# A four-layer megakernel: the last attention's projections copied out in pairs, two kinds of copy fixed to ACT, and roots of variances by bits in the last combine

## The chip, the cores and the metric

The kernel runs on one core of a Trainium2 chip. The metric is device time in microseconds (us) of one execution of the whole program. The time before is 2511.77 us, the median of three runs (2509.81 to 2514.41).

The engines are named as in the profile: PE (matrix products), DVE or VectorE, ACT (ScalarE), POOL (GpSimd) and SP (SyncE, which issues most transfers). PEld is PE's loading of weights, L12 is line 12 of the kernel before.

## What is computed

Four pairs of an attention and a feed-forward layer follow each other over x of 8 blocks x 256 tokens x 256 features, in fp32, each with a residual and a layer norm: `x = _layernorm(x + layer(x))`. The change touches the last pair. Its attention is a differential attention with 16 query heads and 4 key heads:

```
q = _rope((x @ Wq).reshape(b, s, H, 2 * D))
k = _rope((x @ Wk).reshape(b, s, KVH, 2 * D))
v = (x @ Wv).reshape(b, s, KVH, D)
scores = softmax(energy / np.sqrt(D))            # causal, two maps a head
diff = softmax(scores[:, 0] - lam * scores[:, 1])   # causal
att = einsum('bhqv,bvhd->bqhd', diff, v)
att = att * rsqrt(mean(att * att) + EPS) * rms_w * (1.0 - LAM_INIT)
return att.reshape(b, s, E) @ Wo
```

The last feed-forward layer routes each token to 4 of 32 experts (256 to 96 gated to 256), and sums the four results by their weights. Then come the last residual and norm:

```
m = jnp.mean(x); v = jnp.var(x)          # over the 256 features
return (x - m) / jnp.sqrt(v + 1e-5)
```

## The kernel before, in words

The eight blocks of 256 tokens stay in SBUF as `X[b]`, with a transposed copy `xT`. Layers run one after the other. For the last two (`attn3` and `ffn3`) the schedule is manual: each engine takes its instructions in the order in which the code emits them, so whatever stands in an engine's queue waits for all that is ahead of it there.

**Banks.** PSUM is divided by tags, two banks of 128 x 512 fp32 each: "a" and "s" (scores), "o" (attention's values) and "t" (everything else: projections, transposes, the output product). A product for a "t" bank waits until the bank's last content but one was copied out.

**The attention (`attn3`).** `project(b)` makes, for one block, the turned keys and queries and v. Each call of `turn` multiplies 128 columns of a weight with the block's 256 tokens into a "t" bank, and VectorE multiplies the result with a table of cosines or sines (L600). There are four for the keys (POOL adds the two parts of each half, L608), eight for the queries, and one product for v, which VectorE copies to `Vs` (L620). `project` is a generator: after each piece it yields. The first block's runs as a whole before the loop; that of block b + 1 is stepped inside the loop over block b's units.

A block has six units: two with the first 128 queries (qc = 0, two heads each in every group of four) and four with the other 128 (qc = 1, one head each, 256 keys). The loop over units is a software pipeline. In iteration n it emits, in this order:

- `factors` of unit n - 1: the reciprocal of its sums on DVE (L672), masking and the factor c on POOL (L677 to L683);
- `scores` of unit n: 32 or 16 products on PE (L642, two records each in the profile's count), mask products (L655), four maxima on DVE (L659), exponentials on ACT (L662);
- `values` of unit n - 3 on PE (L739); after the last unit of a query half the result is copied from "o" to `oS` by `self.copy`, which alternates between DVE (L118) and ACT (L120) over all its calls;
- one step of the projections;
- the first half of `differences` of unit n - 1: products and sums on DVE (L696), maxima (L700), then POOL (nmd L701, v L704);
- one more step of the projections, two if qc = 0;
- one step of `finish`, the end of an earlier block (transposes L756, att L761, the root mean square with POOL L778 to L788 and ACT L780 and L781, transposes L795, aT on ACT L799, output product L804, residual L164 and moments L183 and L184, norm L190, transposes L154);
- the second half of `differences`;
- one or two steps of the sorting of the last layer's first half, later three scatters on POOL (L954);
- `turned` of unit n - 2: transposes on PE (L721) into "t" and the second exponential on ACT (L723).

**The last layer (`ffn3`).** Tokens go to rows sorted by expert, in two halves of four blocks. The experts' loop runs over 63 tiles of 128 rows a half. `ffn3_combine(g, act, ahead)` then fetches, for each of the 8 tiles of 128 tokens of a half, four results by indirect DMA from POOL (L2048), and VectorE adds them by their weights to `X` (L2054). After each second tile it takes `moments`, and then the norm (L190) and the store of the block (L197). The combine of the first half runs inside the second half's experts; that of the second half runs alone at the end of the program, one tile of gathers ahead of the sums.

`moments` takes mean and variance on VectorE (L183, L184) and calls `rsqrt`, which is two instructions on POOL: multiply and add (L146), and a power of -0.5 (L147).

Of the kernel before, what the change touches and what calls it, by code (L numbers as in the profile page):

```python
# [10 lines left out]
F32 = mybir.dt.float32  # L11
BF16 = mybir.dt.bfloat16  # L12
I32 = mybir.dt.int32
U32 = mybir.dt.uint32
AF = mybir.ActivationFunctionType
ALU = mybir.AluOpType
AX = mybir.AxisListType

P = 128
NB = 8  # L20
T = 256
# [3 lines left out]
LN_EPS = 1e-5  # L25
# [14 lines left out]
class Model:  # L40
# [132 lines left out]
        self.normed(b, r, *self.moments(r))  # L173
        self.norm_done(b)

    def moments(self, r):

        nc = self.nc
        st = self.small.tile([P, 2, 6], F32, tag="bnst", name="bnst")
        mv = self.small.tile([P, 2, 2], F32, tag="bnmv", name="bnmv")  # L180
        rstd = self.small.tile([P, 2], F32, tag="rstd", name="rstd")
        for t in range(2):
            nc.vector.bn_stats(st[:, t, :], r[:, t, :])  # L183
            nc.vector.bn_aggr(mv[:, t, :], st[:, t, :])  # L184
        self.rsqrt(rstd, mv[:, :, 1], 1.0, LN_EPS)
        return mv, rstd

    def normed(self, b, r, mv, rstd):
# [364 lines left out]
    def attn3(self, w, act, keep, start=False, beside=None):  # L553
# [5 lines left out]
        nc = self.nc  # L559
# [4 lines left out]
        for i in range(2):  # L564
            pr = l[:, 2 * i, :]
            nc.vector.tensor_tensor(pr, pr, l[:, 2 * i + 1, :], ALU.mult)
            sm = act.tile([P, 16], F32, tag=f"lsm{i}", name="lsm", bufs=1)
# [17 lines left out]
        def project(b):  # L585

            if start:
                self.transpose_x(b)
            xT = self.xT[b // 2][:, :, (b % 2) * T : (b % 2 + 1) * T]
            qT = act.tile([P, 8, T], F32, tag="qT", name="qT")  # L590
            kT = act.tile([P, 2, T], F32, tag="kT", name="kT")

            def turn(out, wt, i, tab):
                ps = self.ps("t")[:, :T]
                for c in range(2):
                    nc.tensor.matmul(
                        ps, wt[:, c, i * P : (i + 1) * P], xT[:, c, :],
                        start=(c == 0), stop=(c == 1),
                    )
                nc.vector.tensor_tensor(out, ps, tab, ALU.mult)  # L600

            for a in range(2):
                k = kT[:, a, :]
                turn(k, w["wk"], 2 * a, w["ck"][:, a, :])
                yield
                x = act.tile([P, T], F32, tag="kh", name="kh", bufs=1)
                turn(x, w["wk"], 2 * a + 1, w["sk"][:, a, :])
                nc.gpsimd.tensor_tensor(k, k, x, ALU.add)  # L608
                yield
            for j in range(8):  # L610
                turn(qT[:, j, :], w["wq"], j, w["tq"][:, j % 2, :])
                yield
            ps = self.ps("t")[:, :128].rearrange("p (t n) -> p t n", t=2)
            for t in range(2):
                for c in range(2):
                    nc.tensor.matmul(
                        ps[:, t, :], xT[:, c, t * P : (t + 1) * P], w["wv"][:, c, :],
                        start=(c == 0), stop=(c == 1),
                    )
            nc.vector.tensor_copy(  # L620
                Vs[b % 2][:, :, :, 0:16], ps.rearrange("p t (s d) -> p t s d", s=4)
            )
            qTs[b], kTs[b] = qT, kT
            yield

        class Unit:
# [102 lines left out]
            def values(u):  # L729

                V = Vs[u.b % 2]
                if u.h0 == 0:
                    oT[u.b, u.qc] = self.ps("o").rearrange("p (h q) -> p h q", h=4)
                o = oT[u.b, u.qc]
                for c in range(1 + u.qc):
                    for s in range(4):
                        out = o[32 * s : 32 * s + 32, u.h0 : u.h0 + u.nh, :]
                        x = u.p[s] if u.qc == 0 else u.p[s][:, c : c + 1, :]
                        nc.tensor.matmul(  # L739
                            out, V[:, c, s, :], x, start=(c == 0), stop=(c == u.qc)  # L740
                        )
                if u.h0 + u.nh == 4:
                    oS = keep.tile([P, 4, P], F32, tag=f"oS{u.qc}", name="oS", bufs=1)
                    self.copy(oS, o)
                    oSs[u.b, u.qc] = oS
                    if u.qc == 1:
                        done.append(finish(u.b))
# [71 lines left out]
        projections, ends, done = [], [], []  # L819

        def step(queue, n=1):

            while n and queue:
                if next(queue[0], StopIteration) is StopIteration:
                    queue.pop(0)
                else:
                    n -= 1

        for _ in project(0):
            pass  # L830
# [3 lines left out]
        for n in range(len(units) + 3):  # L834

            def at(back):
                return units[n - back] if 0 <= n - back < len(units) else None

            u, last = at(0), at(1)
            if u and u.qc == 0 and u.h0 == 0:  # L840
                step(projections, 100)
                if u.b + 1 < NB:
                    projections.append(project(u.b + 1))
            if last:
                last.factors()
            step(others)
            if u:
                u.scores()
            if at(3):
                at(3).values()  # L850
            step(projections)
            halves = last.differences() if last else iter(())
            next(halves, None)
            step(projections, 2 if u and u.qc == 0 else 1)
            step(ends)
            next(halves, None)
            next(halves, None)
            if not self.scattering:
                step(others, 2)
            if at(2):  # L860
                at(2).turned()
            ends += done
            done.clear()
# [1168 lines left out]
    def ffn3_combine(self, g, act, ahead):  # L2032


        nc = self.nc
        first, n = GROUPS[g]
        wt, slots, _ = self.sorted[g]
        ys, rs = {}, {}
        for t in range(2 * n + ahead):
            i = t - ahead  # L2040
            b = first + i // 2
            if t < 2 * n:
                ys[t] = act.tile([P, 4, D], F32, tag="yk", name="yk", bufs=4)
            if i >= 0 and i % 2 == 0:
                rs[b] = act.tile([P, 2, D], F32, tag="rk", name="rk", bufs=3)
            for k in range(4):
                if t < 2 * n:
                    nc.gpsimd.indirect_dma_start(  # L2048
                        out=ys[t][:, k, :], out_offset=None, in_=self.outs[g],
                        in_offset=bass.IndirectOffsetOnAxis(ap=slots[:, t, k : k + 1], axis=0),  # L2050
                    )
                if i >= 0:
                    r = rs[b]
                    nc.vector.scalar_tensor_tensor(  # L2054
                        r[:, i % 2, :], ys[i][:, k, :], wt[:, i, k : k + 1],
                        self.X[b][:, i % 2, :] if k == 0 else r[:, i % 2, :], ALU.mult, ALU.add,
                    )
                yield
            if i >= 0 and i % 2 == 1:
                m = self.moments(rs[b])  # L2060
                yield
                self.normed(b, rs[b], *m)
                self.norm_done(b)
                yield
# [228 lines left out]
```

## Time and profile before

| what | us |
|---|---|
| median of the three runs | 2511.77 |
| the profiled execution | 2512.97 |
| its span, first to last instruction | 2511.2 |
| the last attention, about | 1745 to 2216 |
| the last layer's experts, about | 2216 to 2452 |
| the last combine and store | 2452 to 2511 |
| PE busy | 2192.5 (87%) |
| DVE busy | 1431.1 (57%) |
| ACT busy | 1047.5 (42%) |
| POOL busy | 916.9 (37%) |

The profile is of one execution. A row of the timeline gives start, duration, engine, line, operation and tiles; in brackets the time that the engine sat idle before it and what ended that. In the table of waits a row names who waited for whom, then the total, the number of times and the longest. The durations of two instructions that follow each other on VectorE overlap a little, so starts tell more than durations. The mean granted clock of PE was 0.949.

### The profile page before, as it was taken

The page shows a single profiled execution, that of the slowest core. Times are in us where ns is not written, and L with a number is a line of the kernel's source. Part 1 is how long each engine was busy: PE and PEld are TensorE (multiplying, and loading weights), DVE is VectorE, ACT ScalarE, POOL GpSimd, SP SyncE. Part 2 cuts the span into 40 slices and gives each one's busy share as a digit, 9 for nine tenths or more (in the row PEclk, how much of TensorE's full clock was granted, in tenths as well). Part 3 has the DMA queues.
Part 4 walks back from the last instruction along what each step waited for, and adds up shares of the span by engine and source line. Part 5 has one row for each costly group of instructions (what it writes and reads, how often), then busy time and mean ns, then how long its engine had stood idle before and what let it go on. Part 6 is the DMA issues. An engine that isn't in the chain of part 4 may idle for free. (4 is left out here: it accounts for less than half of the span.)

```text
span 2511.2 us, 36255 instructions
## 1 busy us (share of the span) xinstructions
PE 2192.5 (87%) x11960; PEld 1494.2 (60%) x12016; DVE 1431.1 (57%) x3593; ACT 1047.5 (42%) x3005; POOL 916.9 (37%) x1725
## 2 busy tenths in 40 slices
PE   7998899999999999999999999998877777678990
PEld 4554697756666666666664465555555554457780
DVE  4556486754544543544465454565888878645463
ACT  1334365453544544544432112221766755644450
POOL 1222443343433323333312321000566557833555
PEclk9999999999999999999999999999999978789995
DMA  5000411100000100000260011002000000145663
GB/s 160 1 1 1 165 44 40 59 5 4 3 3 8 47 1 1 1 1 1 74 206 1 1 51 52 1 0 103 1 2 1 1 1 26 41 125 172 213 212 96
DMA packets 92309, 120.76 MB, mean 48 GB/s; under 512 B 9757, under 2 KB 79582, under 8 KB 91102
## 3 DMA queue, kind: packets, MB, share of 16 engines
q1 hardware_dynamic: 82270, 95.75, 11.8%
q0 software_dynamic: 8192, 21.11, 2.8%
q8 instruction: 100, 1.64, 0.3%
q10 hardware_dynamic: 1664, 1.57, 0.2%
q14 instruction: 83, 0.68, 0.1%
HBM read 67.53 MB, written 50.88 MB: 47 GB/s over the span
## 5 line engine op out<-in xcount | busy, mean ns | idle before, releaser
L1391 POOL TENSOR_SCALAR p<-p,rs 128x128 f32<-128x128 f32 (+1 forms) x256 | 104.2, 425 | 294.7 <-DVE rs L1389 290.4
L1381 ACT ACTIVATE p<-ps_s,nm,rq 128x128 f32<-128x128 f32 (+1 forms) x256 | 128.0, 507 | 152.2 <-DVE nm L1379 152.2
L1309 ACT ACTIVATE sq<-ps_a 128x512 f32<-128x512 f32 x126 | 76.0, 603 | 227.2 <-PE ps_a L1301 226.9
L146 POOL TENSOR_SCALAR rsq<-bnmv 128x2 f32<-128x2 f32 x64 | 13.6, 212 | 377.5 <-DVE bnmv L184 369.9
L662 ACT ACTIVATE e<-ps_a,nm 128x128 f32<-128x128 f32 (+1 forms) x256 | 105.9, 435 | 107.7 <-DVE nm L659 98.4
L1310 DVE TENSOR_REDUCE ssk<-sq 128x4 f32<-128x512 f32 x64 | 43.8, 686 | 172.9 <-ACT sq L1309 172.9
L704 POOL TENSOR_SCALAR v<-e,r,nmd 128x128 f32<-128x128 f32 (+1 forms) x256 | 134.6, 537 | 10.0
L1301 PE MATMUL ps_a<-w_a_wq,xT 128*128 128x512 f32 x256 | 122.3, 600 | 12.4 <-DVE k L1323 9.4
L721 PE MATMUL ps_t<-ident,v 128*128 128x128 f32 x384 | 69.2, 317 | 61.7 <-DVE qT L600 29.4
L1301 PE MATMUL ps_a<-w_a_wv,xT 128*128 128x512 f32 x256 | 120.6, 593 | 1.0 <-ACT q L1334 1.0
L1981 PE MATMUL ps_a<-w_f_gup,xTg 128*128 x504 | 111.5, 345 | 11.4 <-DVE xTg L1975 6.9
L696 DVE SCALAR_TENSOR_TENSOR e<-e,c 128x128 f32<-128x128 f32 (+1 forms) x256 | 105.1, 460 | 25.5 <-POOL c L683 25.3
L1310 DVE TENSOR_REDUCE ssq<-sq 128x4 f32<-128x512 f32 x64 | 43.9, 686 | 129.8 <-ACT sq L1309 129.8
L1301 PE MATMUL ps_a<-w_a_wk,xT 128*128 128x512 f32 x248 | 116.5, 593 | 0.0
L1429 PE MATMUL ps_o<-w_a_wo,attT 128*128 128x256 f32 x512 | 111.8, 379 | 0.0
L662 ACT ACTIVATE e<-ps_s,nm 128x128 f32<-128x128 f32 (+1 forms) x256 | 106.8, 452 | 0.0
L1429 PEld LDWEIGHTS ps_o<-w_a_wo,attT 128*128 128x128 f32 x512 | 96.7, 190 | 12.8
L1163 DVE SCALAR_TENSOR_TENSOR yg<-ps_t,xg,yg 128x128 f32<-128x128 f32 x266 | 93.1, 350 | 12.7 <-PE ps_t L1152 3.9
L1368 PE MATMUL ps_s<-kT,qT 128*128 128x256 f32 (+1 forms) x512 | 100.3, 329 | 0.0
L721 PEld LDWEIGHTS ps_t<-ident,v 128*128 128x128 f32 x384 | 50.2, 163 | 81.4 <-issue 31.4
L1415 PE MATMUL ps_o<-pT,V 128*128 128x256 f32 x256 | 79.5, 392 | 19.2 <-ACT pT L120 19.2
L1981 PEld LDWEIGHTS ps_a<-w_f_gup,xTg 128*128 128x128 f32 x504 | 82.4, 197 | 22.2 <-ACT yg L2011 10.6
(410 smaller groups left out, 6041.7 us busy)
## 6 DMA issues: line engine op xcount, KB each, us to landing
rows<-zero SPq DMA_DIRECT2D x42, 384.0 KB, 4.5
xg<-rows SPq DMA_DIRECT2D x42, 384.0 KB, 5.1
outs<-yg SPq DMA_DIRECT2D x42, 384.0 KB, 3.7
w_f_gup<-in_f_gup SPq DMA_DIRECT2D x8, 768.0 KB, 8.6
w_f_w<-in_f_w SPq DMA_DIRECT2D x8, 512.0 KB, 6.3
w_f_down<-in_f_down SPq DMA_DIRECT2D x8, 384.0 KB, 8.3
w_f_up<-in_f_up SPq DMA_DIRECT2D x5, 512.0 KB, 7.3
lrows<-zero SPq DMA_DIRECT2D x12, 204.0 KB, 5.7
```

Of the source, the lines that this page charges most:

```text
L662: nc.scalar.activation(e[:, s, j * nk : (j + 1) * nk], sc[s][:, j, :], AF.Exp, bias=nm[:, s, j : j + 1], scale=1.0, accum_out=sums[:, s, j ...
L696: nc.vector.scalar_tensor_tensor(d[:, s, h, :], u.e[:, s, h, 1, :], u.c[:, s, h : h + 1], d[:, s, h, :], ALU.mult, ALU.add,)
L704: nc.gpsimd.tensor_scalar(u.v[:, s, h, :], d[:, s, h, :], u.r[:, s, h, 0:1], nm[:, s, h : h + 1], ALU.mult, ALU.add,)
L721: nc.tensor.transpose(ps[:, s, c, :], x, self.ident)
L1163: nc.vector.scalar_tensor_tensor(acc[j], y, c, acc[j], ALU.mult, ALU.add)
L1301: nc.tensor.matmul(ps, self.xt(u.b, t, c), w[which][:, c, u.cols], start=(c == 0), stop=(c == 1),)
L1310: nc.vector.tensor_reduce(out, sq, AX.X, ALU.add)
L1368: nc.tensor.matmul(sc[:, j, :], u.qT[:, h0 + j, qc * P : (qc + 1) * P], u.kT[:, h0 + j, 0:nk], start=(j == 0), stop=False,)
L1381: nc.scalar.activation(u.p[qc][:, h0 + j, :], sc[:, j, :], AF.Exp, bias=nm[:, j : j + 1], scale=r[:, j : j + 1], accum_out=u.sums[qc][:, h ...
L1391: nc.gpsimd.tensor_scalar(u.p[qc][:, j, :], u.p[qc][:, j, :], ri[:, j : j + 1], 1.0, ALU.mult, ALU.mult,)
L1429: nc.tensor.matmul(y[:, t, :], attTs[b][:, h, t * P : (t + 1) * P], w["wo"][:, h, :], start=(h == 0), stop=(h == 15),)
L1981: nc.tensor.matmul(ps, xT[j][:, c, :], w["gup"][:, bass.ds(er[j], 1), c, :].rearrange("p o f -> p (o f)"), start=(c == 0), stop=(c == 1),)
```

## The change

In `project`, `turn` takes several column blocks. It puts two of them side by side into one bank and VectorE multiplies all 512 columns with the two tables in one instruction. So the keys take two steps in place of four (one addition of 512 columns on POOL in place of two of 256), the queries four in place of eight. The loop takes the second step of projections only in units with qc = 0. The copy of v and every copy of `oS` are made by ACT; since `self.copy` alternates, its other calls may fall on the other engine than before. In the last combine the roots are computed by VectorE: a first guess by integer operations on the bits and three Newton rounds, 15 instructions with the addition of eps; only the last block's root stays on POOL.

```diff
+    def rsqrt_bits(self, out, v, eng):
+
+        n = v.shape[1]
+        half = self.small.tile([P, 4], F32, tag="nm", name="rsh")[:, :n].bitcast(I32)
+        self.nc.vector.tensor_scalar(half, v.bitcast(I32), 1, None, ALU.arith_shift_right)
+        self.nc.vector.tensor_scalar(
+            out.bitcast(I32), half, -1.0, float(0x5F3759DF), ALU.mult, ALU.add
+        )
+        t = self.small.tile([P, 4], F32, tag="sm", name="rst")[:, :n]
+        for _ in range(3):
+            eng.tensor_tensor(t, out, out, ALU.mult)
+            eng.tensor_tensor(t, t, v, ALU.mult)
+            eng.tensor_scalar(t, t, -0.5, 1.5, ALU.mult, ALU.add)
+            eng.tensor_tensor(out, out, t, ALU.mult)
+
-    def moments(self, r):
+    def moments(self, r, by_bits=False):
...
-        self.rsqrt(rstd, mv[:, :, 1], 1.0, LN_EPS)
+        if by_bits:
+            v = self.small.tile([P, 4], F32, tag="rs", name="rsv")[:, :2]
+            nc.vector.tensor_scalar(v, mv[:, :, 1], LN_EPS, None, ALU.add)
+            self.rsqrt_bits(rstd, v, nc.vector)
+        else:
+            self.rsqrt(rstd, mv[:, :, 1], 1.0, LN_EPS)
...
-            def turn(out, wt, i, tab):
-                ps = self.ps("t")[:, :T]
-                for c in range(2):
-                    nc.tensor.matmul(
-                        ps, wt[:, c, i * P : (i + 1) * P], xT[:, c, :],
-                        start=(c == 0), stop=(c == 1),
-                    )
+            def turn(out, wt, tab, *cols):
+                ps = self.ps("t").rearrange("p (a t) -> p a t", a=2)
+                for a, i in enumerate(cols):
+                    for c in range(2):
+                        nc.tensor.matmul(
+                            ps[:, a, :], wt[:, c, i * P : (i + 1) * P], xT[:, c, :],
+                            start=(c == 0), stop=(c == 1),
+                        )
                 nc.vector.tensor_tensor(out, ps, tab, ALU.mult)
-            for a in range(2):
-                k = kT[:, a, :]
-                turn(k, w["wk"], 2 * a, w["ck"][:, a, :])
-                yield
-                x = act.tile([P, T], F32, tag="kh", name="kh", bufs=1)
-                turn(x, w["wk"], 2 * a + 1, w["sk"][:, a, :])
-                nc.gpsimd.tensor_tensor(k, k, x, ALU.add)
-                yield
-            for j in range(8):
-                turn(qT[:, j, :], w["wq"], j, w["tq"][:, j % 2, :])
+            turn(kT, w["wk"], w["ck"], 0, 2)
+            yield
+            kh = act.tile([P, 2, T], F32, tag="kh", name="kh", bufs=1)
+            turn(kh, w["wk"], w["sk"], 1, 3)
+            nc.gpsimd.tensor_tensor(kT, kT, kh, ALU.add)
+            yield
+            for j in range(0, 8, 2):
+                turn(qT[:, j : j + 2, :], w["wq"], w["tq"], j, j + 1)
                 yield
...
-            nc.vector.tensor_copy(
+            nc.scalar.copy(
                 Vs[b % 2][:, :, :, 0:16], ps.rearrange("p t (s d) -> p t s d", s=4)
             )
...
-                    self.copy(oS, o)
+                    nc.scalar.copy(oS, o)
...
-            step(projections, 2 if u and u.qc == 0 else 1)
+            if u and u.qc == 0:
+                step(projections)
...
-                m = self.moments(rs[b])
+
+                m = self.moments(rs[b], g == 1 and i < 2 * n - 1)
```

## The prediction

> **What bounds the kernel now.** I read the chain that ended last first, in order of time. It reaches back over the last 300 us only; its end is a run of gathers on POOL, and with the stretch around one root it reads:
>
> ```profile
> 2467.90 0.94 POOL yk L2048
> 2468.84 0.30 issue
> 2469.14 0.94 POOL yk L2048
> 2470.09 0.07 issue
> 2470.16 0.20 POOL rsq L146
> 2470.36 0.07 issue
> 2470.43 0.72 POOL rstd L147
> 2471.15 0.19 issue
> 2471.34 1.17 POOL yk L2048
> 2472.52 0.30 issue
> 2472.82 0.96 POOL yk L2048
> 2473.78 0.31 issue
> 2474.08 0.95 POOL yk L2048
> ```
>
> From 2455 us on, the time is 32 gathers, one every 1.25 us, and three such breaks in between; the last gather starts at 2497.79, lands 2.8 us later, and the last block's norm and store follow. VectorE only has to keep up.
>
> For the other part of the change, the last attention (1745 to 2216 us), I cut the time into stretches: us, then PE, PEld, DVE, ACT, POOL busy, clock, DMA.
>
> ```profile
> 1860.00:1920.00 60.00, 46.31 (x429) 31.93 (x431) 51.63 (x116) 41.29 (x165) 37.77 (x92) 0.97 0.01 2
> 2100.00:2160.00 60.00, 43.08 (x357) 29.51 (x358) 45.91 (x101) 40.23 (x165) 50.89 (x102) 0.86 0.12 40
> ```
>
> To 2100 VectorE is the fullest (86%), PE close behind (77%); then POOL, which also issues scatters, is (85%). Nobody is full, so the waits matter. VectorE's own waits in the stage (total, times, longest) and PE's for a bank that VectorE empties (1800 to 2040 us):
>
> ```profile
> DVE e L696 <- POOL c L683: 25.3, 16, 6.1
> DVE nm L659 <- PE ps_a L655: 16.8, 17, 2.3
> DVE V L620 <- PE ps_t L616: 12.3, 7, 5.2
> DVE res L164 <- PE ps_t L804: 8.8, 5, 1.8
> ```
>
> ```profile
> PE ps_t L721 <- DVE qT L600: 20.9, 16, 2.4
> ```
>
> So PE's in-order queue stands behind the second projection of a unit, which VectorE copies out only after the first half of the differences, and the next scores stand behind that; then VectorE waits for those (16.8 us).
>
> **Tail (roots by bits).** Three of the four roots leave POOL. From the 12th gather's start (2469.14) to the 14th's (2472.82) are 3.68 us, where two periods are 2.50: 1.18 us a root. About 0.1 of that may stay, since the gather beside the norm's two L190 instructions took 1.17 us, and the very first one, with VectorE idle, 1.07. So 1.08 to 1.18, three times: 3.2 to 3.5; I take 3.3. VectorE gets 15 small instructions a block instead (one for eps, two for the first guess, three rounds of four). Small dependent ones start 0.21 us apart in the sorting code (L908 at 2072.87, L909 at 2073.08): 3.2 us a block. Cover: two tiles are gathered in 10.0 us and cost VectorE 8 x 0.51 (L2054) + 1.2 moments + 3.2 + 0.7 (L190) = 9.2. At the end: new last gather at 2456.64 + 30 x 1.25 = 2494.2, landing at 2497.0; the third block's sums end near 2487.5, moments 2488.6, bits 2491.8, norm 2492.5, four sums of tile 6 2494.6, three of tile 7 2496.3. 0.7 us of slack; an instruction of 0.26 us instead of 0.21 would use it up. The last root stays on POOL, where nothing queues behind it: no change.
>
> A rule speaks against this. The row: L2054 reads two SBUF tensors for 0.48 us beside gathers (2464.49, the gather at 2464.16), and the next gather still comes 1.25 us later. The Trainium skill, "SBUF — State Buffer", section "SBUF: two separate sides": VectorE instructions in a two-port mode, or with two SBUF inputs against a GpSimd one that reads SBUF, hold a port pair that GpSimd shares; the loser is blocked, descriptors of POOL's DMAs included, until about 115 ns after VectorE's end (the page's next section). Twelve of the 15 have two SBUF inputs. By the rule (an estimate from that page) 12 x (0.19 + 0.115) = 3.7 us a block would be added where 1.18 is removed: the tail 7.5 us longer. By the row nothing. I take the row, since it is the same engine pair and the same DMA; the other end stays in the range.
>
> **Attention: VectorE's queue.** 84 projections of 256 columns are copied out in the loop (12 for each of seven blocks; the first block's 12 come before it). L600 lasts 0.415 us, but two in a row start 0.33 apart; 512 columns of PSUM (L659) start 0.60 apart. So a pair saves 0.06, 42 pairs 2.5 us, not the 0.14 that durations suggest. V's copy: 7 x 0.25 = 1.8. Half of the 16 oS copies were on VectorE: 8 x 0.60 = 4.8. Sum 9.1 us off VectorE. ACT gets 8 x 0.62 (L120 oS) + 8 x 0.3 = 7.4 us; it waits 98 us for L659's maxima in this stage, and the copies stand behind the unit's 8 or 16 exponentials and ahead of the two of L723. They add a wait on ACT for PE's products, which are done while the exponentials run; behind it queue L723's results, and PE's values for those. Without that cover a copy costs its 0.3 or 0.62 us. A general rule says otherwise (the Trainium skill, "ScalarE: Activation LUTs", "Rules for kernel authors": simple elementwise work belongs on VectorE, up to about three times faster per element in bf16): 3 x 0.68 would be 2.0 us a copy, 16 us on ACT. The rows of oS itself (DVE 680 ns, ACT 586 to 622) decide: fp32 from PSUM is no slower on ACT. POOL's two adds of 0.74 us become one of 512, about 1.4 by the same rate, all of it in a block's first unit; the second half's nmd and v queue behind it, but POOL waits 93 us for L700 in the stage. Uncovered it would be 0.7 us a block.
>
> **Attention: the order.** A unit with one query half (qc = 1) now has one pair, in the first place; qc = 0 has two pairs instead of three turns. Two effects, opposite in sign.
> Later: PE works 1.0 us on a turn (two turns 1891.19 to 1893.18), 2.0 on a pair, and VectorE can't start on half of it. Where VectorE reaches the place, against the end of both turns: 1866.33 / 1866.6, 1874.72 / 1874.8, 1892.81 / 1893.18, and one more like it, 1909.13 / 1909.04. So 0 to 0.4 us, about 0.25 for each of four first places a block: +1.0.
> Earlier: in qc = 1 units nothing of a projection is left after the first half, so PE's turning (1895.21, after 1.21 us of wait) no longer waits for it. I replayed the block from 1863 to 1917 by these rows. The unit from 1872.4 gains 1.3, as its scores come before VectorE needs them (it waited 1.55 there); the next two lose 0.15 and 0.3 (VectorE had no wait to give back, and now waits for a pair); V's unit gains nothing, since VectorE leaves the wait for V at 1901.6 only to wait for POOL's c until 1903.48; the unit with y gains 0.35 less 0.25; the next qc = 0 unit loses 0.5. Sum -0.6, plus half of a copy of oS on average in each place (0.6 a block): -1.2 us a block. What is late next is POOL's c and ACT's loop of exponentials, scores and maxima, about 6.4 us against VectorE's 6.6 in a qc = 1 unit: that is why little more can come. From 2100 us on POOL is the bound and I count nothing. Five blocks: -6.0 us. Ends: -19 (all of the 9.1 and 60% of the 16.8) and +19 (below). I choose near zero because the replayed rows are.
>
> **Sum.** The profiled execution took 2512.97 us around a span of 2511.2; -3.3 - 6.0 makes 2503.7. The median of the runs is 1.2 below that execution: 2502.5. Between the two parts nothing absorbs the gain: the experts' first transfers are issued at 2215.39, when the attention's last instructions are done, and shift with them.
>
> **Rivals.**
> The attention doesn't move: freed VectorE time goes into the waits for POOL's c (25.3 us already) and for pairs. Then only the tail: 2508.5. For it: V's unit above, and POOL after 2100. Against: the unit at 1872.
> The waits dissolve: PE runs ahead, most of L655's and V's waits go, -16 and -3.3: 2492.5. For it: 20.9 us of PE standing behind L600. Against: ACT's loop at 6.4.
> Slower: the pair itself. Its second product makes VectorE wait the full 1.0 us in each of 28 first places and delays the maxima behind it: 28 - 9.1 - 3.3 = +15.6, 2527.4. It decides from 0.44 us uncovered a pair (12.4 / 28), and the replay gave 0 to 0.4; PE's stalls for ACT's p (L739) would bring it there.
> That the edit doesn't do what it says is unlikely: the tags and slots are plain in the code.
>
> **How the numbers follow.** Forecast 0.50 (2502.5, own range 2497 to 2507), dissolving waits 0.17, only the tail 0.18 (with a tail partly eaten by port sharing), slower 0.15. A measurement tells about 0.2%, 5 us, from no change. Faster by more than that is below 2506.7: 0.46 + 0.17 + 0.02 = 0.65; within it 0.16 + 0.04 + 0.01 = 0.21; slower 0.14. The range 2490 to 2516 leaves out most of the slower case and a corner of the fastest.
>
> **What would show it.** Right: no L146/L147 among the last 32 gathers but at the end, 14th gather 2.5 us after the 12th, combine some 3.3 us shorter; L600 x48 in all at about 0.69 us; the stretch 1745 to 2216 about 6 us shorter, all before 2100; no PE wait L721 <- L600 of over 1 us in qc = 1 units. Wrong: a wait L600 <- L596 above 10 us in total (the slower rival), c waits that grow by what VectorE loses, gathers that lengthen beside the bits.

## The result and the profile after

The changed kernel took 2504.79 us in the median of six runs (2501.43 to 2507.46), beside 2514.28 for the kernel before (2509.81 to 2515.04, six runs): a ratio of 0.9965, 95% interval 0.9954 to 0.9976. That is about 9 us less. The profiled execution took 2504.95 us, its span 2502.9.

I cut both spans at four events that both traces have (line numbers of a profile are those of its own kernel, so L2048 before is L2068 after): the first transfer of the experts' weights w_f_gup (the attention follows), the first fetch of sorted rows (the experts follow), the first gather of the last combine, and its last gather.

| stretch, us | before | after |
|---|---|---|
| start to the weights' transfer | 1738.31 | 1739.86 |
| last attention | 477.08 | 472.22 |
| experts | 239.88 | 238.26 |
| last combine, first to last gather | 42.52 | 39.11 |
| last gather to the end | 13.41 | 13.45 |

The experts' 1.6 us count for nothing: that stretch lies between 237.5 and 240.5 us in all profiles but those of one chip (below). The tail first: POOL's timeline of after, with start, duration, line, tiles, and the idle time before each in brackets.

```profile
2465.47 0.95 POOL L2068 DMA_INDIRECT yk<-outs,r_slots  x1 [0.30 <-issue]
2466.72 0.95 POOL L2068 DMA_INDIRECT yk<-outs,r_slots  x1 [0.30 <-issue]
2467.98 1.01 POOL L2068 DMA_INDIRECT yk<-outs,r_slots  x1 [0.30 <-issue]
2469.30 0.95 POOL L2068 DMA_INDIRECT yk<-outs,r_slots  x1 [0.31 <-issue]
...
2489.45 0.95 POOL L2068 DMA_INDIRECT yk<-outs,r_slots  x1 [0.30 <-issue]
2493.96 0.19 POOL L146 TENSOR_SCALAR rsq<-bnmv 128x2 f32<-128x2 f32 x1 [3.56 <-DVE bnmv L199]
```

No root stands between gathers any more; L146 comes once, after the last one. The gather beside the norm (L210) lasts 1.01 instead of 0.95: the small rest that the prediction left in its price. The others keep 1.25 us from start to start, also beside the small instructions.

The attention: the first of the prediction's two stretches, after (us, then PE, PEld, DVE, ACT, POOL busy, granted clock, DMA share and GB/s), and VectorE's waits in the stage (who waits for whom, total, times, longest), then PE's for a "t" bank from 1800 to 2040.

```profile
1860.00:1920.00 60.00, 49.20 (x388) 34.10 (x386) 48.00 (x101) 41.90 (x174) 34.98 (x85) 0.89 0.01 1
```

```profile
DVE e L715 <- POOL c L702: 32.5, 15, 6.1
DVE nm L678 <- PE ps_a L674: 31.2, 23, 3.0
DVE kT L621 <- PE ps_t L617: 12.7, 7, 3.9
DVE qT L621 <- PE ps_t L617: 10.2, 15, 1.3
```

```profile
PE ps_t L740 <- ACT V L639: 10.5, 4, 3.0
...
PE ps_t L740 <- DVE qT L621: 5.4, 5, 1.1
```

VectorE is 3.6 us less busy in that stretch. PE's wait for a projection's copy fell from 20.9 to 5.4 us, but two thirds of what it lost came back as a wait for ACT's copy of v (10.5). On VectorE the waits for POOL's c grew from 25.3 to 32.5 us, for scores from 16.8 to 31.2, and for the products of keys and queries (kT and qT) from 9.3 to 22.9, while the 12.3 us for v's product are gone. So freed time became waiting, and the table's 4.9 us need another source. To find it I measured each block, from its first maximum to the next block's, and block 7 to its own last maximum (times of the rows L659 or L678):

| us | blocks 0 to 4 | block 5 | blocks 6 and 7 |
|---|---|---|---|
| before | 256.1 | 72.9 | 106.4 |
| after | 256.7 | 68.4 | 104.9 |

The steady blocks gained nothing. Block 5 did: the one beside which the gate of the last layer's first half is computed.

### The profile page after: what moved, and what is told of

It is laid out like the page before. It is cut to its first block, busy times and chain, and to the rows that moved or that the text cites. A ratio compares the mean times of both kernels' runs of the same rounds, so it can differ in the third digit from the quotient of the medians.

```text
span 2502.9 us, 36279 instructions
## 1 busy us (share of the span) xinstructions
PE 2198.1 (88%) x12016; PEld 1493.7 (60%) x12016; DVE 1425.6 (57%) x3574; ACT 1050.7 (42%) x3021; POOL 910.7 (36%) x1711
## 5 line engine op out<-in xcount | busy, mean ns | idle before, releaser
L146 POOL TENSOR_SCALAR rsq<-bnmv 128x2 f32<-128x2 f32 x61 | 13.0, 213 | 372.6 <-DVE bnmv L199 365.2
L740 PE MATMUL ps_t<-ident,v 128*128 128x128 f32 x384 | 66.9, 304 | 79.6 <-ACT V L639 19.9
L715 DVE SCALAR_TENSOR_TENSOR e<-e,c 128x128 f32<-128x128 f32 (+1 forms) x256 | 100.6, 443 | 33.0 <-POOL c L702 32.5
L2001 PEld LDWEIGHTS ps_a<-w_f_gup,xTg 128*128 128x128 f32 x504 | 82.5, 198 | 22.7 <-ACT yg L2031 11.0
```

Source lines behind the costliest of these rows:

```text
L715: nc.vector.scalar_tensor_tensor(d[:, s, h, :], u.e[:, s, h, 1, :], u.c[:, s, h : h + 1], d[:, s, h, :], ALU.mult, ALU.add,)
L740: nc.tensor.transpose(ps[:, s, c, :], x, self.ident)
L2001: nc.tensor.matmul(ps, xT[j][:, c, :], w["gup"][:, bass.ds(er[j], 1), c, :].rearrange("p o f -> p (o f)"), start=(c == 0), stop=(c == 1),)
```

## The experiments

Twelve measurements on three chips (numbered 5, 9 and 10 here) take the change apart. The kernel before was measured beside them on each chip: 2522.00 on chip 5, 2512.83 on chip 9, 2513.05 on chip 10. Ratios are to that.

### Chip 5: the parts by themselves

The roots by bits alone, added to the kernel before (of the edit, the call is shown; the function is the change's):

```diff
-                m = self.moments(rs[b])
+                m = self.moments(rs[b], g == 1 and i < 2 * n - 1)
```

> The kernel before with only the roots of the last combine by bits. My theory, by the gathers of the changed profile (first to last gather 39.1 us in place of 42.5): 3.4 us faster than the kernel before, ratio 0.9986. Rival (the port that VectorE and POOL share): the tail gains less than 1 us, because other runs of it lengthen gathers; ratio 0.9996 to 1.000. Second rival: the tail is worth nothing by itself and all of the gain is the attention's.

Measured: 2530.91, ratio 1.0036 (1.0023 to 1.0048), 9 us slower. The gathers took 39.05 us, so POOL gained the forecast 3.4, and gathers lengthened by the first rival, the rule that the prediction set aside, don't show; but from the last gather to the end it was 25.30 us, 12 more. This is VectorE's timeline in the first block's root of that kernel:

```profile
2489.50 0.17 DVE L181 TENSOR_SCALAR rstd<-rsh 128x2 int32<-128x2 int32 x1
2489.87 0.16 DVE L186 TENSOR_TENSOR rst<-rstd 128x2 f32<-128x2 f32 x1 [0.20 <-DVE rstd L181]
2491.26 0.16 DVE L187 TENSOR_TENSOR rst<-rst,rsv 128x2 f32<-128x2 f32 x1 [1.23 <-DVE rst L186]
2491.96 0.17 DVE L188 TENSOR_SCALAR rst<-rst 128x2 f32<-128x2 f32 x1 [0.54 <-DVE rst L187]
2492.16 0.16 DVE L189 TENSOR_TENSOR rstd<-rstd,rst 128x2 f32<-128x2 f32 x1
2493.36 0.17 DVE L186 TENSOR_TENSOR rst<-rstd 128x2 f32<-128x2 f32 x1 [1.03 <-issue]
```

The instructions last 0.16 us as they should, but their starts lie mostly 0.70 or 1.40 us apart where the prediction took 0.21. The stretch of slow starts goes on to 2509.5 and delays the sums behind (L2074), and the 0.7 us of slack are gone; the next block's root has starts 0.20 us apart again. Gathers go on at 1.25 us until their last at 2504.60.

The attention's part alone: the change, with the roots on POOL again.

```diff
-                m = self.moments(rs[b], g == 1 and i < 2 * n - 1)
+                m = self.moments(rs[b])
```

> The changed kernel with all roots of the last combine on POOL as before, so the attention's edits alone. My theory: the rest of the measured gain, 5 us faster than the kernel before (5.3 by the attention's own stretch in the two profiles), ratio 0.998. Rival: that stretch gained by a chance of PE's clock in the sorting of block 5 (7.0 us for the gate products before, 3.8 after), and without that the attention's edits are worth nothing or a loss: ratio 1.000 to 1.002.

Measured: 2519.11, ratio 0.9989 (0.9982 to 0.9995), 2.9 us faster: less than the 5 us expected, and the rival's nothing or a loss is excluded. The attention's stretch is 468.78 us in its profile, beside 474.64 in that of the bits alone, which has the attention before; but this profiled execution took 2515.43, 3.7 us less than the median.

The whole change, but v copied by VectorE as before:

```diff
-            nc.scalar.copy(
+            nc.vector.tensor_copy(
                 Vs[b % 2][:, :, :, 0:16], ps.rearrange("p t (s d) -> p t s d", s=4)
```

> The changed kernel with one part undone: v is copied by VectorE again. Theory A: on ACT that copy stands behind a unit's exponentials and keeps a bank of tag t, and PE's turning waits for it (19.9 us in 7 waits in the changed profile), which costs about 1.8 us in each of 7 blocks, so this version is 8 to 12 us faster than the changed kernel, ratio to the kernel before about 0.992. Theory B: the wait only changes hands, as VectorE then stands before v's product (12.3 us before) and POOL's c comes last anyway: within 2 us of the changed kernel, ratio 0.996 to 0.997. Theory C, what the prediction said: ACT's copy saves VectorE 0.25 us a block: 2 us slower than the changed kernel.

Measured: 2526.13, ratio 1.0015 (1.0008 to 1.0022). The end is 26.04 us, with the same slow starts in the first block's root, so this run tells of the tail, and its three theories about v's copy stay open here; its attention took 470.07 us, 1.3 more than the run above, one profile each.

Pairs and the loop's step alone: `turn` and the loop as in the change, v on VectorE, `oS` by `self.copy`, roots on POOL. Of its edit against the kernel before, the loop's step:

```diff
-            step(projections, 2 if u and u.qc == 0 else 1)
+            if u and u.qc == 0:
+                step(projections)
```

> The kernel before with only the projections in pairs (and the loop's steps that go with them); v and oS are copied as before, roots on POOL. Theory A: the pairs carry the attention's gain, and the copy of v on ACT takes part of it away: 8 to 12 us faster than the kernel before, ratio 0.995 to 0.997. Theory B, by the prediction's replay: the pairs give 0.6 us a block, 3 to 4 us, ratio 0.9985. Slower rival: a pair makes VectorE wait for its second product: ratio above 1.001.

Measured: 2518.65, ratio 0.9989 (0.9981 to 0.9998), 3.4 us faster. That is the size that theory B forecast by the replay (but the blocks below show that it did not come from the replayed ones: 0 to 4 took 258.7 us), and the same as pairs with both copies on ACT. So in time the copies were worth nothing that shows, though the attention's stretch in this profile is 473.61 us where the one with both copies had 468.78.

### Chip 9: is it the chip?

In all four profiles of chip 5 VectorE's product in the experts' stage shows a wait that neither first profile has; the stage took 247 to 250 us there, not 238 to 240. From the waits of the bits-alone run, 2210 to 2460 us:

```profile
DVE h L2010 <- issue: 14.1, 18, 1.4
```

The kernel before, unchanged, with one profile:

> The kernel before, unchanged, for a profile on the chip of this call. Theory C (the slow issue of VectorE goes with the chip): if this chip is like the one of the four runs so far, its median is near 2522, the experts' stage (first fetch of rows to first gather of the last combine) takes 247 to 250 us instead of 239.9, and h waits some 14 to 18 us on 'issue' there; the tail keeps 42.5 and 13.4 us, having no small instructions to slow. Theory P (the slow issue comes from the programs that were changed): the stage stays at 240 and no such wait shows, while the time is still near 2522 for another reason.

Measured: 2511.05 in its one run; experts 238.14 us, no such wait, gathers 42.48, end 13.41. It gives the profile to compare the next with.

The change, unchanged:

> The change, unchanged, measured where the parts were. Theory C: on a chip where VectorE issues slowly in the first block's root the end grows by 12 us as in the runs of the bits alone, so -3.4 -3 +12 makes 1.000 to 1.003 of before (the attention gives 3, the bits cost 9). On a chip without that stretch: 0.9955 to 0.9975, as in the first comparison. Theory D (the slow stretch depends on the rest of the program, since bits alone and bits with the values' copy on VectorE showed it, and the whole change did not): 0.9955 to 0.9975 on either chip, with the end at 13.4 us.

Measured: 2505.43 (eight runs), ratio 0.9972 (0.9962 to 0.9983); experts 237.53, gathers 39.07, end 13.57 us, the attention 468.84 against 473.84. The slow starts aren't there. This fits both theories C and D.

The change with the first block's root on POOL:

```diff
-                m = self.moments(rs[b], g == 1 and i < 2 * n - 1)
+                m = self.moments(rs[b], g == 1 and 1 < i < 2 * n - 1)
```

> The change, but the first block of the last combine takes its root on GpSimd as before; only two blocks take it by bits. If the slow stretch belongs to the place (the first block, some 25 us after the first gather): the stretch meets no small instructions, the end stays near 13.4, gathers take 40.2 us (one root more than after: +1.15), so 0.9960 to 0.9980 whatever the chip. If it belongs to the small dependent instructions, the first root by bits is slow wherever it stands: the end grows by 8 to 12 us again and the ratio is that of the whole change within 0.1%.

Measured: 2505.98, ratio 0.9971 (0.9959 to 0.9983), gathers 40.22 us: one root on POOL is 1.15 us, in the middle of the predicted 1.08 to 1.18. What it was meant to tell, place or kind of instruction, it couldn't, since this chip has no slow stretch.

The two copies alone, without pairs and bits:

```diff
-            nc.vector.tensor_copy(
+            nc.scalar.copy(
...
-                    self.copy(oS, o)
+                    nc.scalar.copy(oS, o)
```

> Before with the two copies on ScalarE alone (V and oS), no pairs, no bits. The prediction's step: V costs 0 to 2 us, oS gives 0.6 a block: 0.9985 to 1.0000. Rival: each V copy stands behind exponentials and holds the product by 0.8 us in two units of each of five blocks, 8 us in all: 1.002 to 1.004. From the difference of the runs with both copies moved (2519.1) and with pairs alone (2518.7): 1.0000 within 0.0008.

Measured: 2514.61, ratio 1.0006 (0.9998 to 1.0015). Taking the copies off VectorE (6.4 us of its busy time, 378.2 to 371.8 over the attention) gains nothing: at most 0.5 us by the interval, where 0.6 a block had been forecast. The 8 us loss of the rival is excluded too, a loss of up to 3.8 is not. The wait for v's product (13.4 us on VectorE in the kernel before on this chip) is gone, and the one for POOL's c took its place, 22.7 us before and 38.0 here:

```profile
DVE e L696 <- POOL c L683: 38.0, 17, 6.5
```

### Chip 10: the bits again, the copy of v again, and block 5

> Before with the three roots by bits alone, measured again. Theory C (the 9 us that it lost were the chip's slow issue of VectorE): on a chip without it, gathers 39.1 us instead of 42.5, end 13.4, so minus 3.4 us: 0.9982 to 0.9990. On a chip with it 1.003 to 1.004 again. If it loses 9 us with an end of 25 us on a chip on which the whole change does not, theory C falls and the slow stretch depends on the rest of the program.

Measured: 2509.83, ratio 0.9986 (0.9979 to 0.9993), 3.2 us faster; gathers 39.10, end 13.49 us. The kernel is the one that lost 9 us on chip 5. The same rows of the same root here, on VectorE:

```profile
2470.61 0.17 DVE L181 TENSOR_SCALAR rstd<-rsh 128x2 int32<-128x2 int32 x1
2470.82 0.16 DVE L186 TENSOR_TENSOR rst<-rstd 128x2 f32<-128x2 f32 x1
2471.01 0.16 DVE L187 TENSOR_TENSOR rst<-rst,rsv 128x2 f32<-128x2 f32 x1
2471.21 0.42 DVE L188 TENSOR_SCALAR rst<-rst 128x2 f32<-128x2 f32 x1
2471.66 0.16 DVE L189 TENSOR_TENSOR rstd<-rstd,rst 128x2 f32<-128x2 f32 x1
```

So the same kernel has the slow starts on chip 5 and not on chip 10: theory D falls, C stands, as far as one slow chip of three can show it; the chip and the time of measuring changed together. Why that chip starts them so, and why in just that root, isn't known. Both kernels with these roots had the stretch in their profile there, and their times without a profile agree with it.

The change with v on VectorE, the same kernel as on chip 5:

> The change with the copy of V back on VectorE, measured again beside the others (the chip of the first look slowed its tail). On a chip without the slow stretch of VectorE: the tail gives 3.4 us; the attention as with pairs and oS on ScalarE. If the V copy on ScalarE cost nothing (the prediction), 0.9965 to 0.9975, the same as the change; if it costs 0.3 us a block (two units later by 0.8 and 1.0 us in some blocks, made good later), 0.9955 to 0.9965. On a chip with the slow stretch: 1.001 to 1.002 as before.

Measured: 2503.94 (five runs), ratio 0.9962 (0.9948 to 0.9975). That is in the range forecast for a copy on ACT that costs 0.3 us a block, but the interval covers the other range too: against 0.9965 and 0.9972 for the change, no difference can be told.

Now block 5. Of its six units, the third differs most: from its first maximum to the fourth unit's takes 16.0 to 16.7 us in four profiles with the attention before, and 11.6 in four with the change's. These are the two maxima, before and after, both on chip 9 (15.97 and 11.58 us):

```profile
2033.27 0.63 DVE L659 TENSOR_REDUCE nm<-ps_a 128x2 f32<-128x512 f32 x1
...
2049.24 0.67 DVE L659 TENSOR_REDUCE nm<-ps_a 128x2 f32<-128x512 f32 x1
```

```profile
2036.47 0.63 DVE L678 TENSOR_REDUCE nm<-ps_a 128x2 f32<-128x512 f32 x1
...
2048.05 0.67 DVE L678 TENSOR_REDUCE nm<-ps_a 128x2 f32<-128x512 f32 x1
```

PE's timeline in that unit, in the same order:

```profile
2036.67 0.66 PE L154 MATMUL ps_t<-ident,X 128*128 128x128 f32 x4 [0.97 <-DVE qT L600]
2038.28 6.35 PE L1909 MATMUL ps_t<-w_f_gate,xT 128*128 128x32 f32 x32 [0.95 <-ACT xT L120]
2044.44 1.09 PE L721 MATMUL ps_t<-ident,v 128*128 128x128 f32 x4
```

```profile
2038.51 0.60 PE L154 MATMUL ps_t<-ident,X 128*128 128x128 f32 x4
2039.53 3.76 PE L1929 MATMUL ps_t<-w_f_gate,xT 128*128 128x32 f32 x32 [0.42 <-DVE qT L621]
2043.13 0.63 PE L740 MATMUL ps_t<-ident,v 128*128 128x128 f32 x4
```

The gate's products (32 records) take 6.35 us before and 3.76 after: 401 and 276 ns each in the median. The granted clock of the stretch 2036 to 2046 is 0.65 before, 0.94 after. Before, they run in a stretch of half clock, and the transposes that the next unit waits for (L721) stand behind them. They also start later before, since X's transposes (L154) wait 0.97 us for the copy of a second projection, which the change has taken out of this unit. In every profile with the whole gate the unit is the sum of three pieces, the third of them 4.61 us (4.74 in the change, where POOL's nmd comes last) from the gate's end to the next maximum:

| us | maximum to gate | gate | unit |
|---|---|---|---|
| before, first profile | 5.01 | 7.02 | 16.64 |
| before, chip 9 | 5.01 | 6.35 | 15.97 |
| copies alone, chip 9 | 5.71 | 7.03 | 17.36 |
| pairs alone, chip 5 | 3.67 | 5.30 | 13.58 |
| the change with v on VectorE, chips 5 and 10 | 3.07 | 4.76, 4.80 | 12.44, 12.48 |
| the change's attention, four profiles | 3.07 | 3.76 | 11.57 or 11.58 |

So on chip 9 the earlier start is 1.9 us and the shorter gate 2.6. Pairs carry most of it; the two copies add to it only together with pairs. The clock falls to half 5.1 and 5.8 us after the unit's first maximum in the two profiles of before, 5.6 with pairs and v on VectorE, and 6.7 to 8.4 with both copies on ACT. Why it falls there, no run shows. To test the gate's part, both kernels got a cut gate: logits from the first of the eight tiles only, used for all eight, so seven eighths of these products are left out and experts are chosen by wrong logits. For the change I took its attention without the bits.

```diff
-        for t in range(n):
+        for t in range(n if each == 1 else 1):
...
+        if each > 1:
+            lg = lg[:, 0, :].unsqueeze(1).to_broadcast([P, n, 32])
```

The kernel before with that cut:

> Before, but the first sorting beside the attention makes the gate's logits of one tile of 128 rows only and uses them for all eight tiles (so the experts are chosen by wrong logits; the number of tiles that the experts work on stays). It removes seven eighths of the gate products that in before run for about 6 us at half the TensorE clock in the third unit of block 5 (16 us from unit to unit there, 8 to 10 in the units ahead). Theory G (the change gained because these products fell into a stretch of full clock): that unit falls to about 10.5 us, the attention gets 5 to 6 us shorter than before, 0.9976 to 0.9982. Theory U (the gain is spread over the units by saved waits): the unit falls too, but the distance to the kernel with the change's attention stays what it was.

Measured: 2508.47, ratio 0.9982 (0.9975 to 0.9989). The unit took 12.0 us instead of 16.0 to 16.6, block 5 took 68.3 instead of 72 to 73, the other blocks stayed (256.2 and 106.6).

The change's attention with that cut:

> The change's attention (pairs, both copies on ScalarE, roots on GpSimd), with the same cut of the gate's logits to one tile of eight. Compared with the run of before that has the same cut: theory G expects the gap between the two attentions to shrink from 4.9 us to about 2 (2.6 to 3 us less, since the products cost 3.8 us at full clock there instead of 6.4), so 0.9965 to 0.9985 against before and at most 0.1% ahead of the other cut kernel. Theory U expects the gap to stay near 5 us, 0.2% ahead of the other cut kernel.

Measured: 2505.75, ratio 0.9967 (0.9955 to 0.9980). The unit took 11.6 us, exactly as with the whole gate. In its place PE now waits; the timeline of this kernel:

```profile
2038.06 0.63 PE L1929 MATMUL ps_t<-w_f_gate,xT 128*128 128x32 f32 x4 [0.43 <-DVE qT L621]
2040.57 0.63 PE L740 MATMUL ps_t<-ident,v 128*128 128x128 f32 x4 [1.88 <-ACT xT L120]
2043.03 1.09 PE L740 MATMUL ps_t<-ident,v 128*128 128x128 f32 x4 [1.83 <-POOL nmd L720]
```

So in the change the gate is covered (POOL's nmd comes last), and before it was not. With the cut the third unit's gap is 0.4 us in place of 4.4 to 5.1. Block 5 takes 68.3 and 68.4 us in the two kernels, and the whole attention 472.68 and 472.24, where the whole gate had 5 between them; here one profile each says less, since block 5 of the uncut change took 68.4 us in one profile and 65.8 in three. The medians are less sharp: 2.7 us between the cut kernels (0.11%, and 0.15% by the ratios, where theory G allowed 0.1), against 2.9 to 6 between the uncut (2.9 on chip 5; 7.4 and 9.5 less the tail's 3.4). So the place is shown by the profiles, and theory G holds for block 5; that the gap in time shrinks by its full size is not resolved.

All blocks of the main runs, as in the table above:

| us | blocks 0 to 4 | block 5 | blocks 6 and 7 |
|---|---|---|---|
| before, chip 9 | 254.1 | 72.2 | 106.9 |
| bits alone, chip 10 | 256.2 | 73.0 | 106.3 |
| the change, chip 9 | 256.3 | 65.8 | 104.7 |
| attention's part alone, chip 5 | 256.2 | 65.8 | 104.7 |
| first root on POOL, chip 9 | 259.7 | 65.8 | 104.7 |
| pairs alone, chip 5 | 258.7 | 69.3 | 104.3 |
| v on VectorE, chip 10 | 257.4 | 68.5 | 103.9 |
| copies alone, chip 9 | 259.7 | 72.2 | 104.8 |

The same attention code gives 256 or 260 us for blocks 0 to 4 in different profiles, so a difference of 3 us between two single profiles says little there. The third unit of block 5 repeats to 0.7 us for the same attention code. The shorter blocks 6 and 7 come with the copies alone as well as with the pairs alone.

## Why the prediction was right, and where it was not

The forecast was 2502.5, the median 2504.8, with -9.5 us against the runs beside it where -9.3 were predicted (and -7.4 on chip 9). The sum is right; one of its two terms is right for its reason, the other isn't.

**Tail, -3.3: right.** Gathers from 42.5 to 39.1 us, the end unchanged, 3.2 us in time for the bits alone on chip 10, 1.15 us a root. Starts were 0.20 us apart where 0.21 was taken, but for one of 0.35 to 0.45 in each root. The choice of the row against the rule was right, and the rule was read too widely. The section that the prediction names in the Trainium skill ("SBUF — State Buffer", "SBUF: two separate sides") speaks of blocked descriptors of POOL's DMAs where VectorE runs in a two-port mode; for two SBUF inputs it has a lock only against a POOL instruction that reads SBUF. The prediction's reading would put some 0.3 us (an estimate from that page) on each instruction with two SBUF inputs, and these are nine a block, as the rows L186, L187 and L189 show, not twelve. Whether one of the other six runs in a two-port mode, no trace shows. The gathers beside them all kept 1.25 us. What failed is the slack of 0.7 us as an assurance. The text said what would use it up, 0.26 us an instruction, and priced the starts from one chip. On chip 5 they were mostly 0.7 or 1.4 us apart in one root, and the bits cost 9 us. The whole change wasn't run there; with v on VectorE it lost 4.1 us, and the sum of its parts (8.9 less 2.9) would be 6 us slower.

**Attention's queue, 9.1 us off VectorE: the size right, the worth zero.** VectorE is 13.4 us less busy in the stage (377.5 to 364.1); 4.5 of that are the sums of L696 (105.1 to 100.6), which the prediction did not count, so 8.9 are left. But the copies alone gave 1.0006. The prediction counted 0.6 us a block for oS; that term measured nothing. Nor did the cost by the general rule against ACT show (16 us by the prediction's estimate from it): with the copies alone ACT was 5.7 us busier (295.9 to 301.5), where 7.4 had been taken.

**V's copy "at nothing": right in time, wrong in the reason.** The sentence was that PE's products are done while the exponentials run. They are, but the copy stands behind the exponentials, and PE then stands for v, 19.9 us in seven waits. In the first block of after, on PE:

```profile
1796.79 1.08 PE L740 MATMUL ps_t<-ident,v 128*128 128x128 f32 x4 [3.85 <-ACT V L639]
```

That first block takes 46 to 47 us with v on ACT and 43 to 44 with pairs and v on VectorE. It isn't lost in the total. Some 0.9 us come back in block 5's third unit (table above); where the rest is made good I didn't isolate.

**Order, -1.2 us a block in five blocks: wrong.** Blocks 0 to 4 took 255.3 us in the mean of four profiles with the attention before (254.1 to 256.2) and 257.2 with the change's (four profiles, 256.2 to 259.7). Three things failed.

- The replay stood on one profile. Its unit from 1872, forecast to gain 1.3, took 9.8 us there, but 7.6, 8.4 and 10.1 in three other profiles of the same attention, and 8.1 to 8.6 in four of the change's. The block's first unit lost 0.8 (10.1 or 10.2 to 10.8 to 11.1), where 0.5 was taken for a unit with qc = 0. In the mean the replayed block took 53.7 before and 54.0 after. (The gains and losses listed there also add up to -0.45 a block, not to -0.6.)
- "About 0.25 for each of four first places a block, +1.0" was too small. Inside the loop VectorE's waits for the products of keys and queries rose from 2.7 to 16.2 us on chip 9: 0.48 for each of the 28 places. That is past the slower rival's own point of decision (0.44). Its loss did not come, because the wait for v's product went at the same time, 13.0 us in the loop: all waits for projections were 15.7 us and are 16.2.
- The time not spent in copies was spent waiting, for c 31.4 us in place of 22.7 and for scores 28.5 in place of 20.7 in the same two profiles.

In these blocks the rival "the attention doesn't move" was the right one. Of the signs named for being wrong, the growing waits for c came true. The other, waits for projections above 10 us, could not tell: they were 11.1 us (kT, qT and kh) in the kernel before.

**"From 2100 us on I count nothing": wrong, -1.8** in blocks 6 and 7 (means of four profiles each, 106.5 and 104.7), and block 5, six us shorter, wasn't in the sum at all. The prediction saw PE's projections stand behind VectorE, but looked at one steady block and not at the one block with an extra load on PE. There the change takes the second projection out of a qc = 1 unit, so X's transposes and the gate start earlier, and the gate is done before or just as the clock falls. The forecast's -6.0 met a measured -4.9 in the stage by luck.

## What to carry to other kernels

When one steady block stands for all in a prediction, look for the blocks in which another stage's work is interleaved: there the queue order decides, and a step taken out ahead of it may be worth more than all steady blocks together. A replay should be laid over a second profile of the same kernel first: a unit that varies by 2 us gives no gain of 1. Freed time on an engine that isn't full is worth what the next wait leaves of it, and a test of that alone (the copies: nothing) is cheap. A chain of small instructions with little slack should be measured on more than one chip before its price is trusted.

## What was unexpected in the hardware

VectorE of chip 5 starts small instructions mostly 0.70 or 1.40 us apart over a stretch of some 20 us, at the same place of the program in both kernels with bits there (24.3 us after the first gather), while their duration (0.16 us) and POOL's gathers stay as elsewhere. Fetching of instructions doesn't explain it: in the kernel with v on VectorE no transfer of the instruction queues falls into the stretch. The experts' stage was some 10 us longer there as well, with 14 to 18 us of idle VectorE that nothing in the profile explains, and the kernel before took 2522 instead of 2513.

The gate's products of 128 x 32 took 276 ns each at full and 401 ns at half clock, so that all 32 took 3.76 us or 7.02. Half clock for some 10 us at the wrong place and a start 1.9 us later made one unit 5.1 us longer.
